# A four-layer graph kernel: the first layer's work one turn earlier, finer pieces of the last layer, and another rule for dealing them

## The chip, the cores and the metric

The kernel runs on one core of one Trainium2 chip. The metric is the device time in microseconds of one execution, start to end. Before the change it is 2979.01 us, the median of three runs (2969.64 to 2980.59). The core's engines are TensorE (PE, matrix products and transposes), VectorE (DVE), ScalarE (ACT), GpSimd (POOL) and SyncE (SP); each works through its own queue in order. SP, ACT and POOL also start DMA transfers.

## What is computed

The input is a batch `x` of 32 graphs of 512 nodes with 256 features each, and one matrix `adj` of 512 x 512 that all graphs share and that is mostly zero. Four layers follow one another:

```python
def gnn(h):                                    # layers 0 and 3, own weights each
    pre_u, pre_v = h @ W1[:256], h @ W1[256:]
    S[u, v] = sigmoid(relu(pre_u[u] + pre_v[v] + b1) @ W2 + b2)
    a = (S * adj).T @ h
    m = (adj.T @ h) * h
    return beta1 * h + beta2 * (a @ Wa + ba) + beta3 * (m @ Wm + bm)

x = gnn(x)                                     # layer 0
x = x + relu((adj @ x) @ W.T + b)              # layer 1
f = x @ W1.T; f1 = f @ W2 + b2                 # layer 2
x = softmax(leaky_relu(f1[:, None] + f1[None, :]) + adj) @ f + bias2 + x
x = gnn(x)                                     # layer 3
```

All of it is float32.

## The kernel before

**Sparse layers 0 and 3.** S is only needed where `adj` is not zero. For each graph `pre` computes pre_u and pre_v and writes them as rows of a table in DRAM. `edges` then fetches rows of the table by index (POOL, L646), adds the partner's row (DVE, L731), takes relu, W2 and the sum (DVE, L739 or L747, or ACT, L717), applies the sigmoid, multiplies by `adj`'s value and puts the results into cells of a dense matrix in DRAM (POOL, L639). `load` brings that matrix back as `SA` (four transfers of 1 MB on POOL's queue, L772).

**Turns and entries.** Four graphs (NB = 4, here called entries) share the fetches of `edges` and make a turn; there are eight turns, 0 to 7. For each turn four streams of work exist:

- `first` (L806): loads a graph (`h`), transposes it (`turned`, L571: PE at L578, ACT copies at L579), stores the transpose as xT, and calls `pre` (PE at L592 and L594, DVE at L596, L599 and L600, ACT at L597, table stores on SP's queue at L604). The edges of layer 0 follow.
- `middle` (the "main" stream): the end of layer 0, then layers 1 and 2, then `pre` for layer 3, entry after entry. Its softmax is at L958 to L964, the transposes of the softmax at L1003.
- `edges` for layer 3.
- `last` (L1094): layer 3's end, of products `hWa` and `mhT` (both through L46), by_S (L1061) and by_Wm (L1073), summed in place into `h` (L1091), and the store of the output.

**The order is written out by hand.** `weave` (L454) takes the streams as generators, each with a list of planned times, one for each piece (the code up to a `yield`), and runs all pieces in order of time. The unit of time is a turn: the main stream of turn t runs from t - 0.47 to t + 0.53, turn 0's from 0 to 0.53. Streams with a list of sizes (`first` and `last`) are treated apart: their pieces are not run when their time comes, but go into the queue `due`. The main stream yields a room at places where its chain will make PE wait, in microseconds: per entry 4.0, 1.7, 1.7, 0.9, 7.0, 3.4, 3.4, 1.7, 1.7, 1.7 and 2.6. At each room, `weave` runs pieces from `due` until the room is used up. They are bound to come behind the main stream's last PE instruction (`issue_after`). If more than HELD = 12 pieces are due, the oldest is run at once, and before `edges` of layer 0 start, all that are due are run. Before the first main stream, pieces run as they come.

**Buffers.** The tile `h` has two buffers, shared by `first` and `last`; `hT` has one, shared in the same way. PSUM, where PE's products land, has seven banks for common use (`psum`, L451). The tile framework decides from the reads and writes of the tiles which instruction waits for which.

Of the kernel before, what the change touches and what calls it, by code (L numbers as in the profile page):

```python
# [8 lines left out]
F32 = mybir.dt.float32  # L9
# [3 lines left out]
ALU = mybir.AluOpType  # L13
# [3 lines left out]
P = 128  # L17
# [19 lines left out]
ITEMS = NC * OWN + 2 * PANELS  # L37
SPARE = NC // 2 * OWN * P + LINES
GROUP = NB * D
HELD = 12  # L40


def mm(nc, out, pairs):
# [360 lines left out]
class Group:  # L404
# [3 lines left out]
    def __init__(self, sp, w, name):  # L408
        self.w = w
        self.table = sp.dram.tile([2 * N, GROUP], F32, name=f"table_{name}")  # L410
        self.cells = sp.cells[name[0]]
        self.layer = name[0]
        self.puts = [f"puts_{name}_{q}" for q in range(2)]
        self.written = [[], []]
        self.s = sp.grp.tile([P, ITEMS, NB], F32, name=f"s{name[0]}")
        self.self_s = sp.grp.tile([P, NC, NB], F32, name=f"self_s{name[0]}")


def by_two(t, n=2):
# [3 lines left out]
class Sparse:  # L423
# [30 lines left out]
    def weave(self, streams):  # L454

        order = []
        for k, (_, times, _) in enumerate(streams):
            order += [(at, k, j) for j, at in enumerate(times)]  # L460
        due, running = [], set()

        def run(k, j):
            g, times = streams[k][:2]
            room = next(g, None)
            if j == len(times) - 1:
                for _ in g:
                    raise AssertionError("more pieces than told")
            return room

        def fill():
            k, j = due.pop(0)
            if running:
                with self.tc.issue_after(self.main):
                    run(k, j)
            else:
                run(k, j)
            sizes = streams[k][2]
            return sizes[j % len(sizes)]

        for _, k, j in sorted(order):
            kind, end = streams[k][2], len(streams[k][1]) - 1
            if isinstance(kind, list):
                due.append((k, j))
                while len(due) > (HELD if running else 0):
                    fill()
                continue
            if kind == "main" and j == 0:
                running.add(k)
            elif j == 0 and kind != "free":  # L490
                while due:
                    fill()
            room = run(k, j)
            if kind == "main":
                self.mark()
                self.main = self.last_of(self.nc.tensor.engine, whole=True)
            while room and room > 0.3 and due:
                room -= fill()
            if kind == "main" and j == end:
                running.remove(k)  # L500
        while due:
            fill()
# [68 lines left out]
    def turned(self, h, name, tag=None):  # L571

        nc = self.nc
        hT = self.act.tile([P, DC, N], F32, name=name, tag=tag or name)
        for c in range(DC):
            pt = self.psum()
            for r in range(NC):
                nc.tensor.transpose(pt[:, r * P : (r + 1) * P], h[:, r, c * P : (c + 1) * P], self.m.ident)  # L578
            nc.scalar.copy(hT[:, c, :], pt)  # L579
        return hT  # L580

    def pre(self, g, b, hT):

        nc, w = self.nc, g.w
        rows = g.table.rearrange("(c p k) (b d) -> p c k b d", p=P, k=2, b=NB)
        for c in range(NC):
            cs = slice(c * P, (c + 1) * P)
            if c % 2 == 0:
                two = [self.psum() for _ in range(2)]
                for k, pp in enumerate(two):  # L590
                    ks = slice((c + k) * P, (c + k + 1) * P)
                    nc.tensor.matmul(pp, hT[:, 0, ks], w["W1"][:, 0::DC, :], start=True, stop=False)  # L592
            pp = two[c % 2]
            nc.tensor.matmul(pp, hT[:, 1, cs], w["W1"][:, 1::DC, :], start=False, stop=True)  # L594
            puv = self.small.tile([P, 2, D], F32, name="puv", bufs=3)
            nc.vector.tensor_tensor(puv[:, 0, :], pp[:, 0:D], w["b1bc"], ALU.add)  # L596
            nc.scalar.copy(puv[:, 1, :], pp[:, D:])  # L597
            both = self.small.tile([P, D], F32, name="both", bufs=1)
            nc.vector.tensor_tensor(both, pp[:, D:], puv[:, 0, :], ALU.add)  # L599
            nc.vector.scalar_tensor_tensor(  # L600
                both, both, 0.0, w["W2bc"], ALU.max, ALU.mult, accum_out=g.self_s[:, c, b : b + 1]
            )
            self.settle()
            self.later = lambda c=c, puv=puv: nc.sync.dma_start(rows[:, c, :, b, :], puv)  # L604
            yield
# [185 lines left out]
            nc.scalar.copy(hWa[:, c : c + 2, :], by_two(pp))  # L791
            yield hWa

    def mhT(self, h, hT, layer, mhT=None):
        nc = self.nc
        if mhT is None:
            mhT = self.act.tile([P, DC, N], F32, name=f"mhT{layer}")
        for c in range(DC):
            pm = self.psum()
            mm(nc, pm, [(h[:, r, c * P : (c + 1) * P], self.m.adj[:, r, :]) for r in range(NC)])  # L800
            nc.vector.tensor_tensor(mhT[:, c, :], pm, hT[:, c, :], ALU.mult)
            yield mhT

    def first(self, g, i):  # L806


        def load(b):
            h = self.act.tile([P, NC, D], F32, name="h0", tag="h", bufs=2)  # L810
            self.nc.sync.dma_start(h, self.xr[i + b])
            return h

        h = load(0)
        for b in range(NB):
            ahead = load(b + 1) if b < NB - 1 else None
            hT = self.turned(h, "hT0", "hT")
            yield
            self.nc.scalar.dma_start(self.xT[i + b], hT)
            yield from self.pre(g, b, hT)  # L820
            h = ahead
        self.settle()

    def middle_before(self, g0, i):
# [184 lines left out]
        return h  # L1009

    def x2T_of(self, i):
        hT = self.act.tile([P, DC, N], F32, name="hT3", tag="hT")
        self.nc.sync.dma_start(hT, self.x2T[i])
        return hT

# [38 lines left out]
            both = slice(c, c + 2)  # L1054
            nc.vector.scalar_tensor_tensor(o[:, both, :], h[:, both, :], w["beta1"], bias, ALU.mult, ALU.add)  # L1055

    def by_S(self, b, c, pz, SA, hWa, alone=False):
        for k in range(2):
            cs = slice((c + k) * P, (c + k + 1) * P)
            for r in range(NC):  # L1060
                self.nc.tensor.matmul(  # L1061
                    pz[:, k * D : (k + 1) * D],
                    SA[r][:, cs, b],
                    hWa[:, r, :],
                    start=(r + k == 0),
                    stop=(alone and k == 1 and r == NC - 1),
                )
# [13 lines left out]
    def sums(self, g, b, h, o, SA, hWa, mhT):  # L1081
        self.scaled(g, h, o)
        halves = []
        for c in range(0, NC, 2):
            pz = self.psum()
            self.by_S(b, c, pz, SA, hWa)
            halves.append(pz)
            yield
        for c, pz in zip(range(0, NC, 2), halves):
            self.by_Wm(g, c, pz, mhT)  # L1090
            self.nc.vector.tensor_tensor(o[:, c : c + 2, :], by_two(pz), o[:, c : c + 2, :], ALU.add)  # L1091
            yield

    def last(self, g, i):  # L1094

        nc = self.nc
        h, hT = self.x2_of(i), self.x2T_of(i)
        SA = self.load(g, 3)
        ahead = self.x2_of(i + 1)
        done = None  # L1100
        for b in range(NB):
            for hWa in self.hWa(g, hT, 3):
                yield
            if done is not None:
                nc.sync.dma_start(self.outr[i + b - 1], done)
                if b < NB - 1:
                    ahead = self.x2_of(i + b + 1)
            for mhT in self.mhT(h, hT, 3):
                yield
            if b < NB - 1:  # L1110
                hT = self.x2T_of(i + b + 1)
            yield from self.sums(g, b, h, h, SA, hWa, mhT)
            done, h = h, ahead
        nc.sync.dma_start(self.outr[i + NB - 1], done)


FIRST_US = [0.9, 2.6, 0.9, 2.6, 0.9]
LAST_US = [1.7, 1.7, 3.4, 3.4, 3.7, 3.7, 1.7, 1.7]


def even(n):
    return [1.0] * n

FIRST, LAST, AHEAD = even(NB * 5 + 1), even(NB * 8 + 1), even(NB * 4 + 1)
ENDS, BEHIND = even(NB * 6 + 1), even(NB * 2 + 1)


# [32 lines left out]
def sparse_path(ctx, m, counts, xr, outr, B):  # L1162
# [10 lines left out]
    for t in range(last + 1):  # L1173
# [7 lines left out]
            first = spread(FIRST, -0.28, -0.06)  # L1181
            edges0 = edge_times(0.02, 0.07, start - 0.06, start - 0.04)
        else:
            first = spread(FIRST, start - 0.82, start - 0.56)
            edges0 = edge_times(start - 0.552, start - 0.505, start - 0.06, start - 0.04)
        edges3 = edge_times(end + 0.003, end + 0.05, end + 0.48, end + 0.54)
        behind = end + 0.56, end + 1.16
        if t == last - 1:
            edges3 = edge_times(end + 0.003, end + 0.05, end + 0.46, end + 0.5)
            behind = end + 0.7, end + 1.06  # L1190
        if t == last:
# [1 line left out]
            edges3 = edge_times(end + 0.003, end + 0.02, end + 0.45, end + 0.46, LEAD_AT_ENDS)  # L1193
            behind = end + 0.29, end + 0.45
        streams += [
            (sp.first(g0, t * NB), first, FIRST_US),
            (sp.edges(g0, ("yT", "mhT0", "hWa0") if t == 0 else ()), edges0, ""),
            (sp.middle(g0, g3, t * NB), spread(middle_shares(t == 0), start, end), "main"),
            (
                sp.edges(g3, *((("yT", "h1", "hT1"), ("mhT0", "hWa0")) if t == last else ())),  # L1200
# [4 lines left out]
        if t == 0:  # L1205
            streams.append((sp.middle_before(g0, 0), spread(AHEAD, -0.15, -0.03), ""))
        if t < last:
            streams.append((sp.last(g3, t * NB), spread(LAST, *behind), LAST_US))
        else:
            streams.append((sp.last_before(g3, t * NB), spread(ENDS, *behind), ""))  # L1210
# [239 lines left out]
```

## Time and profile before

The profiled execution took 2998.45 us, with a span of 2996.8 us on the core; it is a little above the median of the timed runs. The granted TensorE clock was 0.959 of full speed in the mean.

| engine | busy us | share of the span |
|---|---|---|
| PE (matmul) | 2690.0 | 90% |
| DVE | 2307.1 | 77% |
| POOL | 1555.3 | 52% |
| ACT | 1336.8 | 45% |

Cut at the stores of x2T (one at the end of each entry's layer 2), the span falls into these stretches:

| stretch, us | what runs | length | PE busy |
|---|---|---|---|
| 0 to 236 | setup, first layer of turns 0 and 1, edges of turn 0 | 236 | 126.61 |
| 236 to 542 | main stage of turn 0 | 306 | 250.35 |
| 542 to 891 | turn 1 | 349 | 330.41 |
| 891 to 1236 | turn 2 | 345 | 328.82 |
| 1236 to 1582 | turn 3 | 346 | 328.33 |
| 1582 to 1932 | turn 4 | 350 | 330.90 |
| 1932 to 2275 | turn 5 | 343 | 327.50 |
| 2275 to 2613 | turn 6 | 338 | 321.14 |
| 2613 to 2815 | turn 7, its main stage | 202 | 183.14 |
| 2815 to 2997 | tail: edges and end of layer 3 | 182 | 162.76 |

The cuts are a part of an entry apart from the planned borders of the turns, which does not matter for comparing lengths. In such a table, the length less PE's busy time is the time in which PE did nothing; what PE waited for is read from the waits, and where from the timeline.

### The profile page before, as it was taken

The numbers are of one execution on the slowest core, as the hardware profiler recorded it, in microseconds if no ns is written. First come the engines' busy times: TensorE is split into PE (matmuls) and PEld (weight loads), VectorE is DVE, ScalarE is ACT, GpSimd is POOL, SyncE is SP. The second block draws the span as 40 slices with busy tenths as digits, with TensorE's granted clock in tenths as the row PEclk, the third lists the DMA queues.
The fourth block names the chain that finished last, engine by engine and source line by source line (L and its number), as shares of the span: only waits on it lengthen the run. The fifth ranks groups of instructions, "written<-read, shape, count | busy, mean of one in ns | idle before, by whom it ended". The sixth has DMA issues, their size and how long they took to land. (4 is left out here: it accounts for less than half of the span.)

```text
span 2996.8 us, 32453 instructions
## 1 busy us (share of the span) xinstructions
PE 2690.0 (90%) x8645; PEld 1613.9 (54%) x8646; DVE 2307.1 (77%) x6035; ACT 1336.8 (45%) x4101; POOL 1555.3 (52%) x1328
## 2 busy tenths in 40 slices
PE   6367787989998999989999899989999899988998
PEld 3134344545664566546664466646565466644666
DVE  6874786889588885988778885888858896783494
ACT  3553454445344443544344443445434453453262
POOL 2662463646445673556536464466735564361183
PEclk9678998999999999999999999999999999999999
DMA  8875657796678867787677866687677866663474
GB/s 268 286 225 169 213 174 221 233 300 203 217 217 269 268 211 227 230 262 254 209 222 247 275 207 230 216 268 253 211 228 236 303 227 197 208 211 102 148 244 150
DMA packets 302143, 677.30 MB, mean 226 GB/s; under 512 B 52608, under 2 KB 170880, under 8 KB 293760
## 3 DMA queue, kind: packets, MB, share of 16 engines
q0 software_dynamic: 122688, 414.40, 42.9%
q1 hardware_dynamic: 160304, 223.52, 23.0%
q10 hardware_dynamic: 18960, 37.24, 3.4%
q8 instruction: 70, 1.15, 0.2%
q14 instruction: 121, 0.99, 0.1%
HBM read 529.02 MB, written 146.01 MB: 225 GB/s over the span
## 5 line engine op out<-in xcount | busy, mean ns | idle before, releaser
L646 POOL DMA_INDIRECT rows<-table,iv x552 | 679.0, 1230 | 795.5 <-DMA table<-puv 262.7
L639 POOL DMA_INDIRECT cells<-s,cell x576 | 697.6, 1211 | 420.6 <-DVE s L675 243.2
L731 DVE TENSOR_TENSOR rows<-rows,mine 128x1024 f32<-128x1024 f32 x552 | 666.4, 1215 | 101.4 <-DMA rows<-table,iv 72.8
L717 ACT ACTIVATE rows<-rows 128x256 f32<-128x256 f32 x1088 | 439.6, 406 | 445.4 <-DVE rows L739 396.6
L46 PE MATMUL pst<-adj,h 128*128 128x512 f32 x1024 | 452.2, 592 | 0.0
L747 DVE SCALAR_TENSOR_TENSOR rows<-rows,L_gnn_W2bc 128x256 f32<-128x256 f32 x1120 | 414.0, 417 | 1.6
L739 DVE SCALAR_TENSOR_TENSOR rows<-rows,L_gnn_W2bc 128x1024 f32<-128x1024 f32 x272 | 329.4, 1213 | 0.4
L46 PEld LDWEIGHTS pst<-adj,h 128*128 128x128 f32 x1024 | 192.8, 190 | 219.9 <-issue 217.6
L46 PE MATMUL pst<-L_gnn_Wa,hT 128*128 128x256 f32 x1024 | 248.8, 393 | 62.9 <-DMA hT<-xT 57.8
L46 PEld LDWEIGHTS pst<-L_gnn_Wa,hT 128*128 128x128 f32 x1024 | 198.9, 199 | 103.0 <-issue 59.2
L46 PE MATMUL pst<-eT,feats 128*128 128x512 f32 x512 | 237.7, 619 | 10.9 <-ACT eT L1004 10.9
L46 PE MATMUL pst<-adjT,zW 128*128 128x512 f32 x512 | 228.2, 599 | 11.6 <-ACT zW L916 9.7
L596 DVE TENSOR_TENSOR puv<-pst,bc_L_gnn_b 128x256 f32<-128x256 f32 x256 | 104.9, 416 | 162.4 <-DMA table<-puv 89.2
L597 ACT COPY puv<-pst 128x256 f32<-128x256 f32 x256 | 93.2, 371 | 288.1 <-DVE puv L596 225.9
L1061 PE MATMUL pst<-hWa,SA 128*128 128x256 f32 x896 | 220.3, 400 | 0.0
L1061 PEld LDWEIGHTS pst<-hWa,SA 128*128 128x128 f32 x896 | 213.8, 328 | 3.7 <-issue 1.7
L717 ACT ACTIVATION_READ_ACCUMULATOR rows<-rows 128x1 f32 x1088 | 204.7, 188 | 0.0
L860 ACT COPY flat<-SA 128x512 f32<-128x512 f32 x128 | 136.7, 1128 | 136.6 <-issue 62.9
L891 PE MATMUL pst<-flat,hWa 128*128 128x512 f32 x448 | 196.8, 592 | 0.0
L592 PE MATMUL pst<-w_L_gnn_W,hT 128*128 128x512 f32 x256 | 141.5, 681 | 53.9 <-ACT hT L579 36.5
L46 PEld LDWEIGHTS pst<-eT,feats 128*128 128x128 f32 x512 | 99.9, 198 | 133.2 <-issue 113.3
L46 PEld LDWEIGHTS pst<-adjT,zW 128*128 128x128 f32 x512 | 96.5, 191 | 133.4 <-issue 114.0
(176 smaller groups left out, 3984.2 us busy)
## 6 DMA issues: line engine op xcount, KB each, us to landing
table<-puv SPq DMA_DIRECT2D x256, 256.0 KB
SA<-cells POOLq DMA_DIRECT2D x64, 1024.0 KB
h<-in_x_dram SPq DMA_DIRECT2D x64, 512.0 KB
mine<-table SPq DMA_DIRECT2D x64, 512.0 KB
hT<-xT SPq DMA_DIRECT2D x36, 512.0 KB
xT<-hT ACTq DMA_DIRECT2D x32, 512.0 KB
x2T<-yT SPq DMA_DIRECT2D x32, 512.0 KB
x2s<-x ACTq DMA_DIRECT2D x64, 256.0 KB
```

The source lines that it names most:

```text
L46: nc.tensor.matmul(out, lhsT, rhs, start=(n == 0), stop=(n == len(pairs) - 1))
L592: nc.tensor.matmul(pp, hT[:, 0, ks], w["W1"][:, 0::DC, :], start=True, stop=False)
L596: nc.vector.tensor_tensor(puv[:, 0, :], pp[:, 0:D], w["b1bc"], ALU.add)
L639: ins = self.nc.gpsimd.indirect_dma_start(out=g.cells[half], out_offset=bass.IndirectOffsetOnAxis(ap=at, axis=0), in_=s, in_offset=None)
L646: self.nc.gpsimd.indirect_dma_start(out=rows, out_offset=None, in_=g.table, in_offset=bass.IndirectOffsetOnAxis(ap=at, axis=0))
L717: self.behind(nc.scalar.activation(part, part, AF.Identity, accum_out=g.s[:, k, b : b + 1]))
L731: self.behind(nc.vector.tensor_tensor(rows, rows, other, ALU.add))
L739: nc.vector.scalar_tensor_tensor(by_entry, by_entry, 0.0, w2, ALU.max, ALU.mult)
L747: nc.vector.scalar_tensor_tensor(part, part, 0.0, w["W2bc"], ALU.max, ALU.mult, accum_out=at)
L860: self.nc.scalar.copy(flat[:, r, :], SA[r][:, :, b])
L891: nc.tensor.matmul(pz, hWa[:, r, cs], flat[:, r, :], start=(r == 0), stop=False)
L1061: self.nc.tensor.matmul(pz[:, k * D : (k + 1) * D], SA[r][:, cs, b], hWa[:, r, :], start=(r + k == 0), stop=(alone and k == 1 and r == NC ...
```

## The change

- **When the first layer runs.** `first` of turn t is planned from start - 1.82 to start - 1.62 (turn 2: from start - 1.48 to start - 1.28) in place of start - 0.82 to start - 0.56, so its pieces are dealt a turn earlier. `self_s` gets a third buffer for it.
- **Its order.** The loads of the first two graphs are a piece of their own, of size 0. The transposes of entry b + 1 come before `pre` of entry b (not in turn 0, where each comes behind it as before). `hT` gets a second buffer.
- **The last layer's pieces.** `mhT` is split into halves of two products, by_S likewise, so a turn has 50 pieces of at most 1.85 us in place of 33 of at most 3.7. They are planned up to end + 1.0 in place of end + 1.16. The load of the next x2T comes before the current entry's work, and the load of SA becomes a stream of its own, 0.005 before the first piece.
- **The deal.** A piece is run while the room left is over half of its size (before: while the room left is over 0.3). There is no limit on the number of pieces held, and before `edges` of layer 0 only their own `first` must have been run. A first piece of size 0 among the next three is run along with the piece before it.
- **PSUM.** `both` in `pre` is computed in place in the PSUM bank and no longer in a tile in SBUF.

```diff
-HELD = 12
...
-        self.self_s = sp.grp.tile([P, NC, NB], F32, name=f"self_s{name[0]}")
+        self.self_s = sp.grp.tile([P, NC, NB], F32, name=f"self_s{name[0]}", bufs=3)
...
         def fill():
-            k, j = due.pop(0)
...
+            pieces = [due.pop(0)]
+            pieces += [p for p in due[:SIGHT] if p[1] == 0]
+            for p in pieces[1:]:
+                due.remove(p)
+            for p in pieces:
+                if running:
+                    with self.tc.issue_after(self.main):
+                        run(*p)
+                else:
+                    run(*p)
+            return size(*pieces[0])
...
                 due.append((k, j))
-                while len(due) > (HELD if running else 0):
+                while due and not running:
                     fill()
...
-            elif j == 0 and kind != "free":
-                while due:
+            elif j == 0 and isinstance(kind, int):
+                while any(p[0] == kind for p in due):
                     fill()
...
-            while room and room > 0.3 and due:
+            while room and due and room > 0.5 * size(*due[0]):
                 room -= fill()
...
-            both = self.small.tile([P, D], F32, name="both", bufs=1)
-            nc.vector.tensor_tensor(both, pp[:, D:], puv[:, 0, :], ALU.add)
+            both = pp[:, D:]
+            nc.vector.tensor_tensor(both, both, puv[:, 0, :], ALU.add)
...
-            mm(nc, pm, [(h[:, r, c * P : (c + 1) * P], self.m.adj[:, r, :]) for r in range(NC)])
+            for r in range(NC):
+                cs = slice(c * P, (c + 1) * P)
+                nc.tensor.matmul(pm, h[:, r, cs], self.m.adj[:, r, :], start=(r == 0), stop=(r == NC - 1))
+                if fine and r == 1:
+                    yield mhT
...
+        hs, turned = [load(0), load(1)], []
+        yield
+
+        def turn(b):
+            turned.append(self.turned(hs.pop(0), "hT0", "hT"))
+            if b + 2 < NB:
+                hs.append(load(b + 2))
+
+        def kept(b):
+            self.nc.scalar.dma_start(self.xT[i + b], turned[b])
+
+        turn(0)
+        yield
+        kept(0)
         for b in range(NB):
...
+            if b + 1 < NB and not alone:
+                turn(b + 1)
+                yield
+                kept(b + 1)
+            yield from self.pre(g, b, turned[b])
...
-            self.by_S(b, c, pz, SA, hWa)
+            self.by_S(b, c, pz, SA, hWa, ks=(0,))
+            yield
+            self.by_S(b, c, pz, SA, hWa, ks=(1,))
...
+    def load_3(self, g):
+        g.SA = self.load(g, 3)
+        yield
...
+            following = self.x2T_of(i + b + 1) if b < NB - 1 else None
             for hWa in self.hWa(g, hT, 3):
                 yield
...
-FIRST_US = [0.9, 2.6, 0.9, 2.6, 0.9]
-LAST_US = [1.7, 1.7, 3.4, 3.4, 3.7, 3.7, 1.7, 1.7]
+T_US, PRE_US = [0.9], [2.6, 0.9, 2.6, 0.9]
+FIRST_US = [0.0] + T_US + 3 * (T_US + PRE_US) + PRE_US + [0.0]
+LAST_US = [0.0] + NB * (6 * [1.7] + 4 * [1.85] + 2 * [1.7]) + [0.0]
+SIGHT = 3
...
-            first = spread(FIRST, start - 0.82, start - 0.56)
+            ahead = 1.48 if t == 2 else 1.82
+            first = spread(FIRST, start - ahead, start - ahead + 0.2)
...
-        behind = end + 0.56, end + 1.16
+        behind = end + 0.56, end + 1.0
...
-            (sp.edges(g0, ("yT", "mhT0", "hWa0") if t == 0 else ()), edges0, ""),
+            (sp.edges(g0, ("yT", "mhT0", "hWa0") if t == 0 else ()), edges0, len(streams)),
...
+            streams.append((sp.load_3(g3), [behind[0] - 0.005], "free"))
```

## The prediction

> **What bounds the kernel now.** I read the page's busy shares first: TensorE (PE) 90%, VectorE (DVE) 77%, the others near 50%. The chain of waits names work for only a tenth of the span, in the tail, so it says little about a change spread over all turns. I therefore cut the span at the stores of x2T (one per entry), which gives the turns, and asked for busy time per stretch: stretch, length, busy us and count of PE, weight loads, DVE, ACT, POOL, then granted TensorE clock, DMA share, GB/s.
>
> ```profile
> 236.00:542.00 306.00, 250.35 (x729) 134.53 (x728) 213.88 (x560) 144.35 (x393) 130.71 (x118) 0.90 0.61 193
> ...
> 1236.00:1582.00 346.00, 328.33 (x1073) 197.27 (x1072) 282.31 (x767) 154.86 (x465) 188.22 (x160) 0.99 0.73 237
> ...
> 2275.00:2613.00 338.00, 321.14 (x1052) 194.09 (x1051) 269.32 (x730) 148.68 (x448) 180.27 (x152) 0.99 0.71 234
> 2613.00:2815.00 202.00, 183.14 (x558) 103.92 (x557) 116.87 (x318) 82.18 (x207) 67.07 (x60) 0.96 0.41 133
> ```
>
> These are turns 0, 3, 6 and 7. In turns 1 to 6 PE is 95% busy: such a turn lasts as long as its PE work plus some 17 us of gaps. Turn 0 has 56 us of gaps at a clock of 0.90; it has no pieces to fill them. So the change can save only in three ways: close gaps in the full turns, move PE work out of a full turn into an emptier one, or lift the clock.
>
> Next, what PE waits for inside turn 3 (total, times, longest):
>
> ```profile
> PE pst L1003 <- DVE ex L964: 7.0, 4, 3.3
> PE pst L592 <- ACT hT L579: 3.6, 1, 3.6
> PE pst L592 <- DVE both L600: 2.1, 1, 2.1
> PE pst L934 <- DVE yT L923: 1.6, 1, 1.6
> ```
>
> L592 is `pre` directly behind its own transposes; L1003 is the softmax's transpose, the place that rooms are meant to cover. The timeline shows both (start, length, idle before):
>
> ```profile
> 1261.25 1.04 PE L578 MATMUL pst<-ident,h 128*128 128x128 f32 x8
> 1265.89 2.51 PE L592 MATMUL pst<-w_L_gnn_W,hT 128*128 128x512 f32 x4 [3.60 <-ACT hT L579]
> ...
> 1313.38 0.66 PE L1003 MATMUL pst<-ident,ex 128*128 128x128 f32 x4 [3.30 <-DVE ex L964]
> ...
> 1316.82 0.63 PE L1003 MATMUL pst<-ident,ex 128*128 128x128 f32 x4 [1.06 <-DVE ex L964]
> ...
> 1320.83 0.63 PE L1003 MATMUL pst<-ident,ex 128*128 128x128 f32 x4 [1.65 <-DVE ex L964]
> ```
>
> and the stretch around the first gap:
>
> ```profile
> 1262.00:1266.00 4.00, 0.40 (x4) 0.16 (x3) 4.00 (x14) 1.94 (x8) 3.09 (x4) 1.00 0.57 140
> 1266.00:1271.00 5.00, 5.00 (x10) 2.53 (x11) 3.57 (x14) 1.78 (x6) 3.78 (x5) 0.66 0.93 291
> ```
>
> PE stands still for 3.6 us, and for most of the next 5 us works at a clock of 0.66.
>
> **The deal, worked through** from the times, sizes and rooms in the code. A turn has rooms of 29.8 us per entry, 119.2 in all. Before, a full turn's 118.2 us of pieces overfill some rooms by 30.9 us in sum (a 3.7 piece in a room of 0.9) and leave 31.9 us empty: in entry 1 the last three rooms (1.7, 1.7, 2.6: the waits of 1313 to 1321), in entry 2 three more (3.4, 3.4, 1.7). After, 115.7 us of pieces overfill 6.6 and leave 10.1 empty; in entry 1 only the room of 2.6 gets nothing.
>
> **Turns 1 to 5, gaps.** Turning an entry ahead puts pieces and main work between the transposes and `pre`: the waits of 3.6 and 2.1 go, 5.7. Of the 7.0 at L1003, the rooms now filled lie in front of all but a small part: 5. What is late next is L934 behind yT (1.6) and smaller ones, which I leave as they are.
>
> The clock: by the gap rows alone, closing 3.6 us saves 3.6. The Trainium skill (TensorE: Matmul & The Clock Gate, "Why this matters for your kernels") asks for no idle gap over about 3 us, since the clock halves after one. The 0.66 above agrees: 5 us at 0.66 lose 1.7 us. So by the rule this gap costs 5.3, and the run of gaps to 1321 a like 1.7, for the clock dips there too. The rule gives 3.4 a turn on top of 10.7; I take 14.
>
> Against it stands **a new wait**. The second turn of an entry now follows the first with nothing between. Its h needs one of two buffers: one is read by that first turn, the other holds the last layer's sums until their store has landed. In turn 3 the store was issued at 1217.31 and the load that I take to be the next into its buffer at 1220.52, so 3 us pass before the load starts. Its own landing is not listed; the nearest row, the tail's `hT<-x2T` loads of the same size, took 3.5 and 6.8 us. Bounds: 0 (work in between hides it) to about 10 us for each of turns 2 to 5, where the last layer stands in front. Behind the waiting transposes the whole PE queue waits, the main stage too. I take 4, nearest to the shorter load, partly hidden. Over turns 1 to 5: 5 x 14 - 4 x 4 = 54 saved; in round numbers **50**, since turn 1's first entry has empty rooms in both deals.
>
> **Turn 6** loses its first-layer pieces: 118.2 becomes 84.1, 34 us of PE work less. Entry 1 then has nothing in any room. Its price is read from turn 7's entry 1, which is empty today:
>
> ```profile
> 2613.00:2682.00 69.00, 58.16 (x166) 31.82 (x165) 63.03 (x165) 37.70 (x118) 47.01 (x39) 0.90 0.63 197
> ```
>
> 10.8 us of gaps and a clock of 0.90 (about 6 us on 58). So -34 + 17 = -17; the rest of the turn's gaps shrink by a little: **20 saved** (bounds 8 and 34).
>
> **Turn 0** gains 31.6 us of pieces, in entries 0 and 1:
>
> ```profile
> 236.00:297.00 61.00, 50.41 (x138) 26.78 (x137) 25.26 (x63) 23.81 (x52) 11.26 (x12) 0.88 0.47 155
> 297.00:359.00 62.00, 44.92 (x135) 23.71 (x133) 47.45 (x121) 30.80 (x88) 31.53 (x31) 0.89 0.67 212
> ```
>
> These have 10.6 + 17.1 = 27.7 us of gaps, and lose about 11 us to the clock, which filled gaps would give back in part. The fit is loose (8.8 us of pieces in entry 0, 22.8 in entry 1), and every piece brings DVE work: 16 times L596, L599, L600 at some 0.42 us, 21 us, on which the softmax waits. I take **12 lost** (bounds 0 and 31).
>
> **The rest.** `both` in PSUM:
>
> ```profile
> L599 DVE TENSOR_TENSOR both<-pst,puv 128x256 f32<-128x256 f32 x256 | 107.3, 419 | 30.7 <-ACT puv L597 21.5 <-ACT flat L860 0.6 <-issue 0.4
> L600 DVE SCALAR_TENSOR_TENSOR both<-both,L_gnn_W2bc 128x256 f32<-128x256 f32 x256 | 107.3, 419 | 2.8
> ```
>
> 256 is 32 entries by four chunks by two layers. The rows give no price to PSUM: L599 reads it and takes 419 ns, as L600, which doesn't. The Trainium skill (VectorE: DVE Perf Modes, "The TRN2 errata") speaks against the change: a PSUM source costs 120 cycles where SBUF costs 58, and its rules for kernel authors advise copying PSUM out before many operations. By that page an estimate of 62 cycles at its 0.96 GHz, 65 ns, more for each L600, 256 x 0.065 = 17 us of DVE; by the rows nothing. The rows decide; as no row here writes to PSUM from DVE I charge **2** on the path. The write in place must wait for ACT's copy, but L599 waits for L597 already (21.5 us above). The PSUM bank is held through L600, half a microsecond longer, of seven.
>
> Sums in halves and mhT in halves add no instruction. The x2T load goes an entry's work earlier on SP's queue, into a second buffer; PE waits only 5.1 us for it in the whole run, so nothing is booked. The SA load of layer 3 moves from the piece to 0.555 of the turn: the piece was dealt in the same entry, so POOL meets it with the same puts in front. The moved first layer passes SP's and ACT's queues at the same place of a turn, one turn earlier: 4 h loads, 16 table stores, 4 xT stores. In turn 0 they meet a DMA share of 0.61 against 0.73, so I book nothing. POOL's six waits for the table in turns 1 to 6 (127.6 us) may shrink; POOL is half idle. The setup's order changes little: 0, bounds 5 either way. In turn 7 5.3 us of pieces slip from before to behind its end, into a tail with 19 us of PE gaps: 0.
>
> **Sum:** -50 - 20 + 12 + 2 = -56. On the profiled execution's own 2998.45 us (span 2996.8) that is 2942; that execution is 0.65% above the median, so on 2979.01 the forecast is **2923 us**.
>
> **Rivals.** (a) *The gap moves, gain of a third.* L1003 waits for DVE, which is 82% busy in full turns; with PE filled, the softmax may be late behind the edges' 1.2 us operations whatever stands in front, and only the transposes' waits (5 x 5.7 = 28) go, with turns 0 and 6 cancelling: 2951. For it: PE idles at L1003 even in entry 1, after a full room of 7. Against: the waits stand where the deal left rooms empty. (b) *Slower: the h buffer.* Same place as the new wait, larger price: if the load comes behind the table stores queued on SP, PE may stand 25 us in each of turns 2 to 5 (the longest wait for a load of this size, in the setup, is 25.7) with the clock halved after. It decides from (56 + 16) / 4 = 18 us a turn; at 28 it is +40: 3019. Against: today's loads issue within 1 to 3 us of their buffer coming free. (c) *No change:* the program's scheduler orders PE by its own priorities, so the deal's finer fit may not reach the chip: 2975. Against: the gaps of before sit where the deal by hand leaves rooms empty. (d) *More:* all 17 us of gaps close and turn 0 hides all: 2880.
>
> **Chances.** The forecast with 2895 to 2950: 0.52; (d) 0.09; (a) 0.19; (c) 0.08; (b) 0.12. A measurement of this kernel tells 0.5% (15 us) from no change. Faster: 0.52 + 0.09 + 0.19 = 0.80; same 0.08; slower 0.12. The range runs from (d)'s price to the near end of (c): 2880 to 2972.
>
> **What would show it.** Right: turns 1 to 5 near 335 us with PE gaps under 9 and no half-speed stretch at L578; L592 no longer waits for L579; turn 6 near 318; turn 0 near 318 with a higher clock; L600 near 419 ns. Wrong: a PE wait of L578 for `h<-in_x_dram` (b); L1003's wait for L964 unchanged in sum (a); turn 0 over 330.

## The result, and the profile after

The changed kernel takes 3083.28 us in the median of six runs (3070.9 to 3085.49), the kernel before 2974.45 us (2969.12 to 2980.59, six runs): **ratio 1.0358, interval 1.0333 to 1.0383**. It is slower by 109 us, where 2923 us, a gain of 56, was forecast.

The first profiled execution of before was 19 us above the median. The unedited kernel was therefore profiled once more (2982.54 us, span 2980.8), and all accounts below stand against that execution. The two profiles of before differ by 12 us over turns 1 to 5 and by at most 5 us in every other stretch of the table below, so a difference of that size in one stretch says little.

> The kernel before the change, unedited, for a second profile: the first profiled execution lay 19 us above the median. Expected: 2970 to 2985, turns 1 to 6 as in the first profile within 2 us each.

The head of the page of after (busy us, share of the span, count):

```profile
span 3077.1 us, 32246 instructions
PE 2708.2 (88%) x8645; PEld 1631.1 (53%) x8646; DVE 2317.5 (75%) x6035; ACT 1340.1 (44%) x4101; POOL 1549.4 (50%) x1328
```

PE's busy time is 23.5 us above the 2684.7 of before, and the span is 96 us longer. So most of the loss is time in which PE stands. Busy time by stretch shows where. The columns are those of the prediction; the rows are turn 0, turns 1 to 5 as one, and turn 6. After:

```profile
291.00:551.00 260.00, 222.15 (x665) 119.02 (x665) 201.20 (x545) 129.09 (x361) 119.97 (x107) 0.92 0.65 215
551.00:2359.00 1808.00, 1659.78 (x5340) 1002.08 (x5339) 1418.28 (x3825) 776.99 (x2315) 950.06 (x803) 0.97 0.69 227
2359.00:2692.00 333.00, 298.01 (x979) 183.85 (x978) 257.76 (x679) 143.00 (x425) 182.12 (x155) 0.97 0.68 218
```

Before, profiled again:

```profile
292.00:536.00 244.00, 200.19 (x593) 108.31 (x592) 188.67 (x498) 120.50 (x342) 119.51 (x107) 0.90 0.64 204
536.00:2257.00 1721.00, 1639.79 (x5367) 988.68 (x5366) 1410.82 (x3823) 777.27 (x2316) 959.70 (x800) 0.99 0.73 239
2257.00:2593.00 336.00, 321.93 (x1053) 194.75 (x1052) 269.09 (x730) 148.88 (x450) 179.91 (x152) 0.98 0.71 236
```

These cuts lie at the store of x2T of each turn's first entry, so the stretches are not those of the prediction's table; lengths are compared only between rows cut alike. To a tenth of a microsecond the sum is:

| stretch | before | after | difference | gaps of PE before, after |
|---|---|---|---|---|
| ahead of turn 0 | 292.0 | 291.4 | -1 | |
| turn 0 | 244.3 | 259.5 | +15 | 43.8, 37.8 |
| turns 1 to 5 | 1720.5 | 1808.4 | +88 | 81.2, 148.2 |
| turn 6 | 336.5 | 332.5 | -4 | 14.1, 35.0 |
| turn 7 | 197.4 | 189.1 | -8 | |
| tail | 190.1 | 196.3 | +6 | |
| span | 2980.8 | 3077.1 | +96 | |

The loss lies in the full turns: 67 us of new gaps, and 21 us by which nearly the same PE work (5340 and 5367 instructions on record) takes longer, at a clock of 0.97 where it was 0.99. What PE waits for in turns 1 to 5 of after (total us, times, longest):

```profile
PE pst L583 <- DMA h<-in_x_dram: 43.4, 4, 11.4
PE pst L959 <- DVE yT L948: 31.1, 18, 3.5
PE pst L1028 <- DVE ex L989: 24.7, 4, 7.4
PE pst L937 <- DVE hT L924: 16.4, 5, 5.4
PE pst L597 <- DVE yT L1006: 13.0, 5, 2.6
PE f L975 <- ACT feats L967: 11.9, 7, 3.0
```

The same in before (the change moved the lines: L578 became L583, L592 L597, L912 L937, L934 L959, L950 L975, L1003 L1028):

```profile
PE pst L592 <- ACT hT L579: 29.6, 10, 5.2
PE pst L1003 <- DVE ex L964: 25.1, 18, 3.2
...
PE pst L934 <- DVE yT L923: 4.0, 4, 2.1
```

Four things are to be seen. The waits of `pre` for its own transposes, 29.6 us, are gone as forecast. A wait of 43.4 us in four times, once in each of turns 2 to 5, has come for the input `h`. L959, which waited 4.0 us for DVE's yT, now waits 31.1; and L937 and L975, two more products of the main chain, wait 28.3 us where they had waited 0.6. L1028 waits as long for `ex` as before, but in 4 places, not 18.

**The wait for h**, in turn 4. PE's timeline (start, length, then the idle time before it and what ended it):

```profile
1620.08 1.04 PE L583 MATMUL pst<-ident,h 128*128 128x128 f32 x8
1631.83 1.94 PE L583 MATMUL pst<-ident,h 128*128 128x128 f32 x8 [10.72 <-DMA h<-in_x_dram]
1633.56 8.95 PE L45 MATMUL pst<-eT,feats 128*128 128x512 f32 x16
```

SP's queue over the same time:

```profile
1619.33 0.39 SPq L1145 DMA_DIRECT2D out_dram<-h  x1
1621.15 13.03 SPq L820 DMA_DIRECT2D h<-in_x_dram  x3
```

The last layer's output store, from one of the two buffers of `h`, is issued at 1619.33; the first load of `h` in the row of three follows at 1621.15, and the second transposes start at 1631.83. All of PE's queue stands behind them, the main stage too. SP's own waits from 1615 to 1640 us name the transposes twice and the store once:

```profile
SPq L820 <- DMA out_dram<-h: 4.9, 1, 4.9
SPq L820 <- PE pst L583: 3.4, 2, 2.1
```

The load that PE waits for is issued right behind the first transposes (1620.08 + 1.04 = 1621.12), 5.3 us before the store lands at 1626.47; so it waited for the buffer that these transposes read. The time from the issue to the landing (L820, 1615 to 1632 us):

```profile
DMA to landing us min/median/max: 10.6/10.6/10.6
```

The wait is thus almost the whole flight of one load: 10.3 to 11.2 us in the four turns. Then PE works slowly (by stretch):

```profile
1621.00:1632.00 11.00, 0.28 (x3) 0.20 (x2) 1.61 (x9) 3.20 (x13) 5.82 (x6) 0.63 0.92 334
1632.00:1642.00 10.00, 10.00 (x24) 5.24 (x24) 2.89 (x3) 2.48 (x8) 0.99 (x1) 0.73 0.46 161
```

At a clock of 0.73 over 10 us, 2.7 us more are lost. Over turns 1 to 5 the time with the clock at half grew from 37.5 to 126.3 us, PE's gaps included.

**The wait for yT**, in the rooms behind zW, y and f. PE and DVE around one of them, each in its own timeline:

```profile
1503.38 2.01 PE L1086 MATMUL pst<-hWa,SA 128*128 128x256 f32 x8
1505.92 2.00 PE L959 MATMUL pst<-WT,yT 128*128 128x257 f32 x8 [0.53 <-DVE yT L948]
1511.35 3.56 PE L959 MATMUL pst<-WT,yT 128*128 128x257 f32 x8 [3.42 <-DVE yT L948]
```

```profile
1505.78 1.22 DVE L736 TENSOR_TENSOR rows<-rows,mine 128x1024 f32<-128x1024 f32 x1
1508.77 1.23 DVE L736 TENSOR_TENSOR rows<-rows,mine 128x1024 f32<-128x1024 f32 x1 [1.77 <-DMA mine<-table,iu]
1510.61 0.68 DVE L948 TENSOR_TENSOR yT<-yT,hT 128x512 f32<-128x512 f32 x1
```

The room behind y is told as 1.7 us, and the new deal put exactly one half of by_S into it (2.01 us on PE). But yT's second half stands in DVE's queue behind an addition of the edges, which itself waits 1.77 us for fetched rows. The true wait is the piece and the two gaps, 2.01 + 0.53 + 3.42 = 5.96 us, over three times the room.

### The profile page after: what moved, and what is told of

Its sections match the earlier page's. It is cut to its first block, busy times and chain, and to the rows that moved or that the text cites. A ratio compares the mean times of both kernels' runs of the same rounds, so it can differ in the third digit from the quotient of the medians.

```text
span 3077.1 us, 32246 instructions
## 1 busy us (share of the span) xinstructions
PE 2708.2 (88%) x8645; PEld 1631.1 (53%) x8646; DVE 2317.5 (75%) x6035; ACT 1340.1 (44%) x4101; POOL 1549.4 (50%) x1328
## 5 line engine op out<-in xcount | busy, mean ns | idle before, releaser
L651 POOL DMA_INDIRECT rows<-table,iv x552 | 660.9, 1197 | 880.6 <-ACT rows L722 161.9
L644 POOL DMA_INDIRECT cells<-s,cell x576 | 714.1, 1240 | 354.2 <-DVE s L680 180.6
L601 DVE TENSOR_TENSOR puv<-pst,bc_L_gnn_b 128x256 f32<-128x256 f32 x256 | 105.8, 416 | 150.0 <-DMA table<-puv 88.4
L1028 PE MATMUL pst<-ident,ex 128*128 128x128 f32 x512 | 88.5, 303 | 94.3 <-DVE ex L989 64.9
L1006 DVE SCALAR_TENSOR_TENSOR yT<-pst,col_L_gnn_bias,yT 128x512 f32<-128x512 f32 x64 | 47.7, 746 | 160.7 <-PE pst L45 160.4
L959 PE MATMUL pst<-WT,yT 128*128 128x257 f32 x512 | 130.1, 403 | 42.7 <-DVE yT L948 42.7
```

The source lines that it names most:

```text
L644: ins = self.nc.gpsimd.indirect_dma_start(out=g.cells[half], out_offset=bass.IndirectOffsetOnAxis(ap=at, axis=0), in_=s, in_offset=None)
L651: self.nc.gpsimd.indirect_dma_start(out=rows, out_offset=None, in_=g.table, in_offset=bass.IndirectOffsetOnAxis(ap=at, axis=0))
L959: nc.tensor.matmul(pn[:, 0 : D + 1], yT[:, r, ic * P : (ic + 1) * P], m.WT_2[:, r, :], start=(r == 0), stop=(r == DC - 1),)
```

## The experiments

The ratio, and the difference of the medians beside it, are to the kernel before as measured with each group of runs (2974.45 us with after, 2979.54 with E1 to E4, 2978.0 to 2978.1 with the rest).

| kernel | median us | against before, us | ratio (interval) |
|---|---|---|---|
| after | 3083.28 | +109 | 1.0358 (1.0333 to 1.0383) |
| E1 after, transposes behind `pre` | 3032.24 | +53 | 1.0153 (1.0109 to 1.0196) |
| E2 after, old rule of the deal | 3009.89 | +30 | 1.0086 (1.0061 to 1.0111) |
| E3 E1 and E2 | 3000.55 | +21 | 1.0062 (1.0048 to 1.0076) |
| E4 before, new rule alone | 3061.95 | +82 | 1.0256 (1.0215 to 1.0298) |
| E5 before, first layer a turn earlier alone | 2996.31 | +18 | 1.0050 (1.0029 to 1.0071) |
| E6 before, halves alone | 3032.93 | +55 | 1.0189 (1.0151 to 1.0226) |
| E7 E1 with wider rooms | 2966.01 | -12 | 0.9958 (0.9935 to 0.9980) |
| E9 after with wider rooms | 2983.78 | +6 | 1.0008 (0.9989 to 1.0027) |
| E10 E7, first layer at its old time | 2954.89 | -23 | 0.9931 (0.9913 to 0.9949) |
| E11 before with wider rooms | 2987.71 | +10 | 1.0033 (1.0017 to 1.0048) |
| E12 E10 with five `puv` buffers | 2948.22 | -30 | 0.9895 (0.9861 to 0.9930) |

**Which part loses: E1, E2, E3.** Two theories stood: the new wait for `h` (rival (b)), and the deal that uncovers the main chain's own waits. E1 puts each transpose behind `pre` again, in all turns:

```diff
-            (sp.first(g0, t * NB, t == 0), first, FIRST_US),
+            (sp.first(g0, t * NB, True), first, FIRST_US),
```

> The changed kernel, but in every turn the transposes of entry b + 1 come behind pre of entry b, as before the change. Theory 1 (the second transposes of a turn wait for the buffer of h and its load, 10.5 to 11.4 us in four turns, with the clock halved after): the L583 wait for h<-in_x_dram goes to 0, and the time falls by 4 x (11 + 2 to 4), so 50 to 60 us, to about 3028; the wait of pre behind its own transposes (some 4 to 6 us a turn) comes back and takes 20 to 30 of it: 3045 to 3055. Rival, theory 2 (the deal fits rooms too closely; the main chain's own waits are longer than the rooms say): the h wait is swallowed by the next room, within 1% of 3083.

E2 brings back the rule of the deal:

```diff
-            while room and due and room > 0.5 * size(*due[0]):
+            while room and room > 0.3 and due:
```

> The changed kernel, but a piece is dealt while the room left is over 0.3, as before the change. Theory 2 (overfilled rooms covered waits of the main chain that are longer than the rooms): L959 behind yT falls from 6.5 to about 2 us a turn, L1028 by some us, and the time by 6 to 10 us a turn in six turns: 3025 to 3045. Theory 1: only the place of the h wait can move; under 15 us either way.

E3 does both.

> Both edits of the two runs before together. If theories 1 and 2 each hold a share, their gains add: about 2990 to 3010, near the kernel before the change. If one of them is only the other's shadow, no better than the better of the two alone.

By the differences, E1 saves 56 us of the 109 and E2 79, each more than expected, but both together save 88, not 135. The parts overlap, and E2's waits say where. In its turns 1 to 5:

```profile
PE pst L959 <- DVE yT L948: 10.6, 10, 3.1
PE pst L959 <- DVE rows L752: 10.4, 3, 3.7
...
PE pst L583 <- DMA h<-in_x_dram: 7.9, 4, 2.0
...
PE pst L959 <- DVE s L624: 4.2, 3, 2.0
```

E2 shortens the wait for `h` from 43.4 to 7.9 us, although the transposes stay ahead, but L959's only from 31.1 to 25.2 (the three rows together; two of them name the edges' work, which stands on the same DVE queue). By the deal worked out by hand, the room behind y gets one half of by_S under both rules, and the old rule ends the previous turn's last layer three rooms sooner. So most of what E2 gives back is the wait for `h` and what follows it. E1, which has no wait for `h`, leaves L959 where it was:

```profile
PE pst L959 <- DVE yT L948: 38.2, 18, 3.6
```

So both losses are real, and the wait for `h` is in large part a consequence of the deal. In E3 L959 waits 8.2 us only, though the room behind y still gets the same half: how late yT is also depends on what else stands on DVE, and no run takes that apart. Of the 21 us that remain in E3, its trace has 19.5 in turn 0 (263.8 us), as E5 below has 22.

**Each part alone on the kernel before: E4, E5, E6.** E4 takes over the rule only:

```diff
-            while room and room > 0.3 and due:
+            while room and due and room > 0.5 * streams[due[0][0]][2][due[0][1] % len(streams[due[0][0]][2])]:
```

> The kernel before the change with one edit: a piece is dealt while over half of it fits. Theory 2: slower by 20 to 50 us (2995 to 3025), with more waits at L934 behind yT and L1003 behind the softmax. Theory 1, or that the rooms are right: within 15 us of 2975.

It costs 82 us, more than expected, with waits of which before has little (10.0 us for zW and 4.0 for yT over turns 1 to 5). In E4, from 600 to 2600 us:

```profile
PE pst L934 <- DVE yT L923: 40.4, 13, 5.0
PE pst L46 <- ACT zW L916: 25.4, 6, 5.4
```

A whole piece of 3.4 or 3.7 us is not under twice 1.7 or 0.9. So, worked out by hand, the rooms behind zW, y and f get no piece of the last layer at all: the uncovering in its purest form. (The limit of 12 held pieces then runs some of them outside the rooms; what that costs was not tried apart.) E5 plans the first layer earlier:

```diff
-            first = spread(FIRST, start - 0.82, start - 0.56)
+            ahead = 1.48 if t == 2 else 1.82
+            first = spread(FIRST, start - ahead, start - ahead + 0.26)
```

(and `self_s` has its three buffers.)

> The kernel before the change with one edit: the first layer's pieces are planned a turn earlier (and self_s has three buffers for it). Theory: the shift costs turn 0 some 12 to 15 us and gives turn 6 back 10 to 20: within 10 us of 2979. Rival: the shift itself is a large part of the loss (pieces in turn 0 delay its softmax on VectorE, and turn 6 gives nothing back): 2995 or more.

It costs 18 us, which this theory had not expected. Turn 0 grows from 244.3 to 266.3 us; turn 6 gives back 14 (336.5 to 322.3), turns 1 to 5 stay (1720.8). E6 cuts the pieces in halves:

```diff
-LAST_US = [1.7, 1.7, 3.4, 3.4, 3.7, 3.7, 1.7, 1.7]
+LAST_US = 6 * [1.7] + 4 * [1.85] + 2 * [1.7]
...
-            self.by_S(b, c, pz, SA, hWa)
+            self.by_S(b, c, pz, SA, hWa, ks=(0,))
+            yield
+            self.by_S(b, c, pz, SA, hWa, ks=(1,))
```

(and `mhT` in halves.)

> The kernel before the change with one edit: mhT and by_S of the last layer in halves, with their sizes. Theory 2: the coarse pieces overfilled the rooms at zW, y and f by up to 2.8 us and covered the main chain's true waits there; with halves the old rule overfills less, so L934 behind yT and L46 behind zW wait longer: 2985 to 3000. Rival: size of pieces is neutral under the old rule, or finer is better: 2970 to 2980.

It costs 55 us, more than expected, with the same signs in a milder form: 25.8 us in 11 waits for yT and 16.3 in 8 for zW, from 600 to 2600 us. Under the old rule a room of 1.7 is now full after one half; before, it took a whole piece of twice its size. The limit of 12 held pieces also holds less work when pieces are halves; what part of the 55 us is due to that was not tried apart. It may be a large one: E3 has the same halves and the old rule without that limit, beside other changes, and loses only 21.

**The rooms themselves: E7, E9, E11.** If the old overfilling was useful, then what is wrong is the size that the rooms are told as. E7 is E1 with those rooms doubled:

```diff
-            yield 1.7 * (d == DC - 1)
+            yield 3.4 * (d == DC - 1)
...
-            yield 1.7 * (c == DC - 1)
+            yield 3.4 * (c == DC - 1)
...
-                    yield 0.9 * (r * ic > 1)
+                    yield 1.7 * (r * ic > 1)
```

> The changed kernel with the transposes behind pre (as in the first run) and the rule of over half kept, but the rooms behind zW and y told as 3.4 us in place of 1.7 and the one behind f as 1.7 in place of 0.9. Theory 2 (these rooms are smaller than the chain's true waits): against the first run's 3032 the wait of L959 behind yT falls from 45 us to under 20 and the time by 20 to 35 us, to 2997 to 3012, near the run with the old rule. Rival (the rule hurts by what it leaves for later, not by these rooms): no better than 3025, the waits move to the rooms that now stay empty.

It takes 2966.01 us, 65 less than E1 when each is set against its own runs of before (20 to 35 were expected), and is faster than the kernel before. In its turns 1 to 5 L959's wait fell from 38.2 us to

```profile
PE pst L1028 <- DVE ex L989: 21.5, 11, 3.7
PE pst L959 <- DVE yT L948: 10.6, 6, 3.0
```

E9 is after with the same three edits and nothing else, the transposes still ahead:

> The changed kernel with the wider rooms of the run before (3.4 behind zW and y, 1.7 behind f), but its transposes ahead by an entry, as changed. Theory 1: the wait for h stands where the last layer's sums end two rooms before the transposes that need its buffer; the wider rooms end them earlier, so L583 waits under 3 us a turn and the time is within 12 us of the 2966 with the transposes behind. If the order itself costs (more work of VectorE in one place), it is slower than 2985.

2983.78 us: **three numbers give back 103 of the 109 us that after has lost.** Its waits in turns 1 to 5:

```profile
PE pst L1028 <- DVE ex L989: 28.7, 14, 3.6
PE pst L959 <- DVE yT L948: 17.8, 11, 2.6
PE pst L583 <- DMA h<-in_x_dram: 8.8, 4, 2.5
```

The wait for `h` has all but gone here too. Its loads at L820 in turns 1 to 5 landed fast, where the trace tells the landing:

```profile
DMA to landing us min/median/max: 3.8/3.9/5.3
```

In turn 4, moreover, 2.3 us of the main stage's products stand between the first transposes and the second. The order of the transposes still costs 18 us (E9 against E7). E11 is the control: the wider rooms on the kernel before, with its coarse pieces and old rule.

> The kernel before the change with the wider rooms alone. Theory 2 says that its coarse pieces overfill these rooms already, so a truer number changes little: within 10 us of 2978. If the wider rooms alone bring 12 us or more, the gain of the earlier run is theirs and not that of pieces and rooms fitting together.

There they bring nothing (+10 us), as expected: pieces of 3.4 and 3.7 filled those rooms already. So wider rooms are no gain by themselves; they repair what the new deal broke.

**A version that beats both: E10, E12.** E10 is E7 with the first layer planned as before (start - 0.82 to start - 0.56).

> Wider rooms, transposes behind pre, and the first layer planned as before the change (one turn later again), the rest as changed. From the run with the shift alone (+18 us) and the 19 us by which turn 0 is longer: turn 0 back to some 245 us, turn 6 up by 13, time 2950 to 2962. Rival (the shift costs nothing under the new deal): 2966 within 5.

It saves 11 us more (the intervals of the ratios overlap a little): turn 0 is back at 243.5 us, at the price of turn 6 (337.8). E12 gives `puv` five buffers for three; for the space, `hT` has one again.

```diff
-            puv = self.small.tile([P, 2, D], F32, name="puv", bufs=3)
+            puv = self.small.tile([P, 2, D], F32, name="puv", bufs=5)
```

> As the run with wider rooms and the old plan, with five buffers for puv in place of three, and one for hT in place of two to make the space. If VectorE's stand at L601 for the table's store (up to 7.3 us in the changed kernel, with the softmax queued behind it) counts, the wait of L601 for the table falls to near 0 and the time by 5 to 15 us. If it is cover for nothing, or hT's one buffer costs as much, within 5 us.

The reason to try it lay in the trace of after. DVE, then PE:

```profile
1340.98 0.69 DVE L984 SCALAR_TENSOR_TENSOR ex<-ex 128x512 f32<-128x512 f32 x1
1349.01 0.42 DVE L601 TENSOR_TENSOR puv<-pst,bc_L_gnn_b 128x256 f32<-128x256 f32 x1 [7.33 <-DMA table<-puv]
```

```profile
1350.37 1.09 PE L1028 MATMUL pst<-ident,ex 128*128 128x128 f32 x4 [7.11 <-DVE ex L989]
```

`pre` is dealt into a room of the softmax; its fourth chunk needs a `puv` whose table store has not landed, and the softmax's own steps stand behind it on DVE. With five buffers, L601's wait for the table stores over the whole run fell from E10's first row below to E12's second:

```profile
DVE puv L601 <- DMA table<-puv: 66.3, 35, 5.9
```

```profile
DVE puv L601 <- DMA table<-puv: 0.3, 1, 0.3
```

and L1028's wait for ex in turns 1 to 5 from 15.5 to 4.0 us. The time fell by 7 us; the intervals of the two ratios overlap, so this last step is likely and not certain. L937's wait for hT rose at the same time from 7.2 to 27.7 us; whether the single buffer of `hT` did that was not tried apart. At 2948.22 us, **E12 is 1.05% faster than the kernel before** (interval 0.70 to 1.39%).

## Why the prediction was wrong

**The step that failed** is "the deal, worked through", with the line that booked the main chain's other waits at nothing: "What is late next is L934 behind yT (1.6) and smaller ones, which I leave as they are." The deal's sums are right, but the prediction counted the 30.9 us of overfilled rooms as work in the wrong place. In turns 1 to 5 PE waited 4.6 us for z, yT and f (L937, L959 and L975 of after) with the old deal and 59.4 with the new: 55 us for which nothing was booked. Two comparisons without any wait for `h` show that the deal opens such waits: E4 (the rule alone loses 82 us, L934 waits 40.4) and E7 against E1 (wider rooms save 65 us, L959 falls from 38.2 to 10.6). E9 shows on the changed kernel itself that the room numbers give back 103. L937's part was not tried apart, and E3 shows that a full room is not all that keeps yT on time. None of the rivals named this step. The profile of before could have warned of it: the deal put 3.7 us in the room behind y, told as 1.7, and PE still waited there, if little; a room twice overfilled without idle time in front of the next step gives no reason to call the excess waste.

**The new wait, "I take 4", bounds 0 and 10.** It measured 43.4 / 4 = 10.9 us a turn, just past the upper bound, and half speed behind it, of which the bounds took no account. The mis-sized term is the load: 3.5 to 6.8 us were read from the tail, and 10.3 to 11.2 came, with an output store and an xT store of some 7 us each under way and a DMA share of 0.92. In E9, at a share of 0.64, the like load took 3.9. What makes the flight longer was not tested apart. Undoing the order (E1) saves 56 us, 14 for each of turns 2 to 5. Rival (b) thus had the place, and the sign that it named (L578, now L583, waiting for `h`) came true, but neither its price, which decides from 18 us a turn, nor its cause: SP issues no table store between the output store and the load. And the wait is not the transposes' alone: with the old rule or the wider rooms it is 7.9 or 8.8 us in all four turns, near 2 each, below the 4 that was taken.

**"Turns 1 to 5: 50 saved"** became 88 lost. Inside it, the waits for the transposes' copies did go (29.6 us, forecast 5 x 5.7 = 28). The 5 of 7 us a turn at L1003 did not: 25.1 us before, 24.7 after. The rooms in front were filled, and the count fell from 18 to 4, but the four that came in are long (5.0 to 7.4 us, in entry 1 of turns 2 to 5). Each ends just behind a `puv` stall of DVE such as the one above (L601 stands 5.3 to 7.6 us for the table's store): DVE work in front of the softmax, as rival (a) feared. E12, with more buffers, is the one run where this wait nearly goes. The gain of 3.4 a turn from the clock turned round: the time at half clock rose by 89 us.

**Turn 0, "12 lost"**: 15 in after, 22 in E5; the pieces went in at nearly full price, as PE's gaps shrank only from 43.8 to 37.8. **Turn 6, "20 saved"**: 4 in after, 14 in E5. PE has 25 us less to do there, and 21 us of new gaps. 17.6 of them are one wait at L1028 in entry 1, the entry that was forecast to be empty; its gaps had been priced at 10.8 from turn 7. So moving the first layer earlier has no gain: E5 says that it costs 18 us, and E10 against E7 points the same way with 11. **The tail, 0**: 6 us longer. The 5.3 us of pieces that slip into it would account for that, but the cause was not tested; the tail is also 203.1 us long in E4, with no halves at all, and 186.9 in E5.

**`both` in PSUM, "I charge 2".** A row that the prediction did not look at decides. After:

```profile
L604 DVE TENSOR_TENSOR pst<-pst,puv 128x256 f32<-128x256 f32 x256 | 108.6, 430 | 39.3 <-ACT puv L602 35.8
L605 DVE SCALAR_TENSOR_TENSOR pst<-pst,L_gnn_W2bc 128x256 f32<-128x256 f32 x256 | 107.9, 429 | 2.1
L605 DVE DVE_READ_ACCUMULATOR pst<-pst,L_gnn_W2bc 128x1 f32 x256 | 35.9, 140 | 0.0
```

and the last of these in before:

```profile
L600 DVE DVE_READ_ACCUMULATOR both<-both,L_gnn_W2bc 128x1 f32 x256 | 20.6, 80 | 0.0
```

The two operations are 11 and 10 ns longer (419 before), and the read of the sum behind them 60 ns. In all that is 0.081 us x 256 = 21 us of DVE over the run. The estimate of 65 ns for each L600, 17 us in all, by the Trainium skill (VectorE: DVE Perf Modes, "The TRN2 errata") was near the 70 ns by which L605 and its read grew, and taking the operations' own rows as "no price" was the error. What it costs on the path was not tried.

**What was right:** the turn's PE work as its floor, the removal of the waits at L592, the signs of turns 0 and 6, and the clock rule: in turns 1 to 5 of after, all 16 gaps of 2.8 us and more have the clock at half in them or just behind, and none of the nine from 1.2 to 2.0 us has. The sizes in the code sum to 115.6 and 84.0 where the prediction has 115.7 and 84.1, which changes nothing.

**What stays open:** a third buffer for `h`, `puv` with five buffers beside two of `hT`, `both` in SBUF within E12, why the load of `h` took over 10 us, and what besides the rooms makes yT late.

## What to carry to other kernels

When filler work is dealt into rooms, the rule, the size of the pieces and the room numbers are one setting: a rule that overfills can hide that a room is told at half its true wait, and a finer or more exact deal then uncovers it, so measure the wait of each room with nothing in it first. Look at places with little idle time as closely as at the gaps: ask what covers them today, and whether the change takes it away. A piece dealt ahead brings its buffers and its DVE work with it; it blocks an in-order queue, and the main chain behind it, as soon as one of its buffers is late.

## What the hardware showed unexpectedly

The read of an accumulator behind an operation that reads and writes PSUM took 140 ns, against 80 ns behind the same operation reading and writing SBUF, while the operation itself changed by 10 ns only; which of the two ends counts, no run separates. A gap of 10.7 us of PE cost more than itself: the clock stood at 0.73 for 10 us of full work behind it, so four such gaps and the smaller ones stretched nearly the same products of turns 1 to 5 by 21 us in all. And a load of 512 KB took 10.6 us at a DMA share of 0.92, where the like load took 3.9 at 0.64.
